# A piece of layer 1 moved behind the weight sums in TensorE's order (graph attention, two layers, one core)

## The chip, the core and the metric

The kernel runs on one core of a Trainium2 chip. A core has a matrix engine (TensorE, PE in the profile; its weight loads are the row PEld), a vector engine (VectorE, DVE), a scalar engine (ScalarE, ACT), GpSimd (POOL) and SyncE (SP), which here issues transfers, and 16 DMA engines. The engines run beside each other, each through its own list of instructions in order; they wait for each other on semaphores. The metric is the device time of one execution in microseconds (us); lower is better.

## What is computed

`x` is 4096 x 512, `adj` a 4096 x 4096 matrix of zeros and ones. Two graph layers follow, each with a residual and a layer norm:

```python
# layer 0: graph attention, 8 heads of 64
feats = einsum('nf,hfo->hno', x, W)
dense = leaky_relu(s_self[:, :, None] + s_neigh[:, None, :], 0.2) * A
out   = einsum('hij,hjo->hio', softmax(dense), feats) + b
x     = layernorm(x + relu(out as 4096 x 512))
# layer 1: attention inside 32 graphs of 128 nodes
scores = (where(mask, q @ k.T * scale, 0) + adj + adj) * where(mask, 1, -1e6)
x      = layernorm(x + (softmax(scores) * mask) @ v)
```

## The kernel before

**Layer 0 as a stream.** The exponential of a leaky ReLU of a sum is one of two products, so a weight can be had from a maximum of two terms. The kernel passes over the transposed adjacency four times, `main_pass(r)` with r = 0 to 3, two heads in each. A pass has four chunks c = 0 to 3 of 1024 rows, a chunk 32 tiles j of 128 neighbours. The tiles go in cycles: 8 tiles a cycle in passes 0 to 2 (`wide=8`), 4 in the last pass (r = 3). Chunks and cycles are numbered from 0 here. For each j and head, DVE makes `q` (line 1369, 128 x 1024), and ACT (line 1378) or, once in four tiles, DVE (line 1374) makes `mark`, which says on which side of the maximum an entry lies.

A cycle on PE is, in the order of the code:

- `accf` (line 1389): the products of the adjacency tile with the features f ("A f"), 16 matmuls for 4 tiles;
- a first call of `pieces`, place 0 (only where r > 0);
- `acc` (line 1409): the products of `q` with the scaled features g ("Q g"), 64 matmuls for 4 tiles, four side by side on 32 columns each;
- a second call of `pieces`, place 1;
- `dens` (line 1423): the weight sums from the marks, 32 matmuls for 8 tiles, so only in cycles that end on a multiple of 8;
- in pass 0 `ae` (`sums_over_a`, line 1333), and then the rest of the adjacency tiles of the next cycle (`bring`): in pass 0 transposes on PE into a `ps_m` bank (line 1115), copied out by ACT (line 1119) and written to DRAM by POOL; in later passes a load on SP's queue (line 1105).

**Pieces.** Other work on PE is cut into generators and run at these two places. When a chunk ends, `sums_to_rows` takes the sums out (DVE lines 1163 and 1171 empty `accf` and `acc`, ACT line 1173 copies `dens`) and gives a generator that turns them into rows. In passes 0 to 2 `run_pieces` steps it: in pass 0 at place 1, in passes 1 and 2 at place 0. For pass 0 it has three steps with PE work: `pz` (4 transposes, line 1186, read by DVE lines 1191 and 1197), `pd` (line 1220, read by line 1223) and `fin` (8 transposes into two banks, line 1243, read by line 1244).

In the last pass, from chunk 1 on, `run_plan` steps layer 1 itself for the blocks of the chunk before, by a plan written out by hand (lines 1277 and 1278). In its strings E is the generator of the chunk that ended, a and b are the two blocks of 512 rows, R loads the rows of the second, F ends a layer norm. The plan of cycle g is a pair, place 0 and place 1:

```python
PLAN = [("E", "b"), ("b", "Fb"), ("b", "a"), ("Ra", "a"), ("Fa", "b"), ("ba", "b")]
PLANS = PLAN + [("ab", ""), ("aaba", "")], PLAN + [("a", ""), ("aa", "a")]
```

`layer_1` has nine steps: two of transposes of the rows (line 960, copied to `x1T` by ACT, line 961); two of zT = M x (line 980, sixteen matmuls each, copied by ACT line 987); the scores (line 1007) with their softmax; values 0 and 1 (line 1052) with a transpose between; rows out (line 1066, then DVE line 1068 and a layer norm); values 2 and 3 (line 1052, sixteen matmuls, read by DVE line 1060); rows out.

**Order and buffers.** Only PE's order is the order of the code; for the other engines a planner fixes the order when the program is built, from the order of the code and its own estimate of when operands are ready:

```python
ctx.enter_context(tc.manual_schedule(engines={mybir.EngineType.PE}))
```

PSUM has eight banks: `acc` 2, `accf` 2, `dens` 1; in pass 0 `ae` 1 and two `ps_m` banks that all pieces and `bring` share in turn, later three `ps_m` banks. `q` has 8 buffers in passes 0 to 2, 6 in the last; marks have 18.

Of the kernel before, what the change touches and what calls it, by code (L numbers as in the profile page):

```python
# [404 lines left out]
def adjacency_streamed_path(  # L405
# [152 lines left out]
    def ring(name, pool, n):  # L558

        if name not in more:  # L560
            return pool
        k = turns[name] % (n + more[name][1])
        turns[name] += 1
        return pool if k < n else more[name][0]
# [536 lines left out]
    def bring(r, c, j):  # L1101

        if r:
            at = ats[r, c, j] = ring("at", atp, 6).tile([P, C], F32R, name="at")
            nc.sync.dma_start(at.bitcast(F32), at_d[c, j])
            return
        if j % 2:
            return
        if j % 4 == 0 and (c, j) not in a_bs:
            load_adjacency(c, j)  # L1110
        pairs = a_bs[c, j - j % 4].rearrange("p t n -> p (t n)").bitcast(BF16)
        pairs = pairs.rearrange("p (t k n) -> p t k n", t=CT, k=2)[:, :, j % 4 // 2, :]
        pt = misc([P, CT, P], BF16)
        for t in range(CT):
            nc.tensor.transpose(pt[:, t, :], pairs[:, t, :], ident_b)  # L1115
        both = pt.rearrange("p t n -> p (t n)").bitcast(FP8).rearrange("p (n k) -> p n k", k=2)
        for k in range(2):
            at = ats[r, c, j + k] = ring("at", atp, 6).tile([P, C], F32R, name="at")
            nc.scalar.copy(at, both[:, :, k])  # L1119
            nc.gpsimd.dma_start(at_d[c, j + k], at.bitcast(F32))  # L1120

    def load_block():

        k = len(checked)
        per = N // CK
        if k < per * NT:
            ck = ckp.tile([P, CK], F32, name="ck")
            nc.sync.dma_start(ck, adj[ts(k // per, P), ts(k % per, CK)])
            checked.append(ck)
# [151 lines left out]
    def run_plan(todo, pinned=False):  # L1281
        for k in todo:
            if k == "F":
                plan[k](pinned)
                continue
            gen = ends[0] if k == "E" else plan[k]
            if gen is not None:
                next(gen)
            if k == "E":
                ends.pop(0)  # L1290
# [3 lines left out]
    def run_pieces(budget):  # L1294

        state["credit"] += budget
        while state["credit"] > 0.0 and (work or ends):
            queue = ends or work
            try:
                state["credit"] -= next(queue[0])  # L1300
            except StopIteration:
                queue.pop(0)
        if not (work or ends):
            state["credit"] = 0.0
# [3 lines left out]
    def main_pass(r, ae=None, wide=4):  # L1308

        for c in range(NCH):  # L1310
# [10 lines left out]
            def pieces(c, group, place):  # L1321
                if r == PR - 1 and c:
                    run_plan(PLANS[c == NCH - 1][group][place])
                elif place == (r == 0):
                    run_pieces(0.75 * wide)
# [18 lines left out]
            for j0 in range(0, NT, wide):  # L1344
                at_step = steps.index((r, c, j0))
                cycle = range(j0, j0 + wide)
                f_s, g_s = {}, {}
                for k in range(j0 // 4, (j0 + wide) // 4):
                    f_s[k] = fsp.tile([P, 4, 2, FP], F32R, name="f_s")
                    nc.sync.dma_start(  # L1350
                        f_s[k].rearrange("p u s n -> p (u s n)").bitcast(F32), f_d[r, k]
                    )
                    g_s[k] = gfp.tile([P, 4, 2, FH], F32, name="g_s")
                    nc.sync.dma_start(g_s[k].rearrange("p u h o -> p (u h o)"), g_d[r, k])
                if at_step == 0:
                    for j in cycle:
                        bring(0, 0, j)
                follow = [
                    x
                    for x in steps[at_step + wide : at_step + 2 * wide]  # L1360
                    if x[0] == r or x[0] < PR - 1 or x[2] < 4
                ]
                qs = {}
                for j in cycle:
                    for h in range(2):
                        hh = 2 * r + h
                        q = qs[j, h] = ring("q", qp, 6).tile([P, C], F32, name="q")
                        d_j = d_all[:, j, hh : hh + 1]
                        nc.vector.scalar_tensor_tensor(  # L1369
                            q, p_row[h], d_j, ats[r, c, j].bitcast(F32), op0=OP.max, op1=OP.mult  # L1370
                        )
                        mark = marks[j, h] = sgp.tile([P, C], FP8, name="mark")
                        if j % 4 == 3 and h == 1:
                            nc.vector.tensor_scalar(  # L1374
                                mark, q, d_j, None, op0=OP.is_gt, saturate=False
                            )
                        else:
                            nc.scalar.activation(  # L1378
                                mark,
                                q,  # L1380
                                AF.Sigmoid,
                                bias=nb_all[:, j, hh : hh + 1],
                                scale=BIG,
                                saturate=False,
                            )
                for j in cycle:
                    for w in range(2):
                        for s in range(2):
                            nc.tensor.matmul(  # L1389
                                accf[:, s, :],  # L1390
                                f_s[j // 4][:, j % 4, w, :],
                                ats[r, c, j][:, ts(s, HB)],
                                start=(j == 0 and w == 0),
                                stop=(j == NT - 1 and w == 1),
                            )
                if r == 0 and (c, j0 + wide) == (NCH - 1, NT):

                    sums_over_a(c, cycle)
                first = wide // 2 if r == 0 or wide == 4 else 6
                for x_ in follow[:first]:  # L1400
                    bring(*x_)
                if r:
                    pieces(c, j0 // 4, 0)

                for j in cycle:
                    for s in range(2):
                        for o in range(0, FP, 32):
                            h = o // FH
                            nc.tensor.matmul(  # L1409
                                acc[o : o + 32, s, :],  # L1410
                                g_s[j // 4][:, j % 4, h, o % FH : o % FH + 32],
                                qs[j, h][:, ts(s, HB)],
                                start=(j == 0),
                                stop=(j == NT - 1),
                            )
                pieces(c, j0 // 4, 1)

                done_j = j0 + wide
                for j in range(done_j - 8, done_j) if done_j % 8 == 0 else ():
                    for s in range(2):  # L1420
                        for h in range(2):
                            lo = 32 * (2 * s + h)
                            nc.tensor.matmul(  # L1423
                                dens[lo : lo + 6, :],
                                e_b[:, j, 2 * r + h, :],
                                marks[j, h][:, ts(s, HB)],
                                start=(j == 0),
                                stop=(j == NT - 1),
                            )
                if r == 0 and (c, j0 + wide) != (NCH - 1, NT):  # L1430
                    sums_over_a(c, cycle)
                for x_ in follow[first:]:
                    bring(*x_)
                group_0 = (at_step - NT * NCH) // 4
                for group in range(group_0, group_0 + wide // 4) if r else ():
                    if group == 0:
                        load_block()
                        load_block()
                    for _ in range(1 + (group % 3 == 2)):
                        check_block(done[0])  # L1440
                        done[0] += 1
                        load_block()
# [16 lines left out]
    with tc.tile_pool(name="wl1", bufs=1, side="right") as wp:  # L1459
# [4 lines left out]
        for gen in work:  # L1464
            for _ in gen:
                pass
        work.clear()
    main_pass(2, wide=8)
    more.clear()
    wide_passes.close()  # L1470
# [60 lines left out]
```

## Time and profile before

| what | us |
|---|---|
| three runs | 2071.25, 2072.22, 2074.30 |
| median | 2072.22 |
| the profiled execution, its own time | 2073.38 |
| its span, first to last instruction | 2071.1 |
| pass 0 to pass 2, start to end | about 169 to 1366 |
| last pass, chunk 0 | 1366 to 1462 |
| last pass, chunks 1 to 3, and the tail | 1462 to 1952, 1952 to 2071 |

The busy shares of the engines and the granted clock of PE in parts of the execution:

| from : to | PE busy | DVE busy | ACT busy | clock |
|---|---|---|---|---|
| 316 : 343 (a cycle of pass 0) | 26.66 | 22.07 | 23.06 | 1.00 |
| 1366 : 1462 | 96.00 | 89.92 | 87.02 | 1.00 |
| 1462 : 1631 | 167.36 | 127.11 | 118.75 | 1.00 |
| 1631 : 1802 | 170.64 | 127.72 | 110.01 | 1.00 |
| 1802 : 1952 | 150.00 | 114.05 | 95.78 | 1.00 |

A row of a timeline is: start in us, length in us, engine, line, operation, what is written from what, shape, and how many are merged (x16). A bracket gives the idle time of the engine before it and whose result ended it. Matmul records overlap, so the time that a block of them takes on PE is read from its own start to the start of the next block.

### The profile page before, as it was taken

To read this page: it belongs to the slowest core of one execution; us is meant where nothing else is said; L and a number is where in the kernel's file an instruction comes from. 1 tells how busy PE (TensorE), PEld (TensorE's weight loads), DVE (VectorE), ACT (ScalarE), POOL (GpSimd) and SP (SyncE) were. 2 spreads that over 40 slices of the span, in tenths; PEclk is the share of its full clock that TensorE was granted. 3 is DMA by queue.
4 is the path that set the end of the run, shared out by engine and by line. 5 is a ranking of instruction groups with operands and counts; after the bars stand their busy time and mean duration, and the time that the engine had idled before them with its cause. 6 is when DMAs were issued, how large, how long until landed. Compare 5 with 4: busy or idle time off the path is not lost.

```text
span 2071.1 us, 37984 instructions
## 1 busy us (share of the span) xinstructions
PE 2038.5 (98%) x14934; PEld 1000.2 (48%) x14934; DVE 1664.2 (80%) x2058; ACT 1536.9 (74%) x1821; POOL 249.3 (12%) x393
## 2 busy tenths in 40 slices
PE   8999999999999999999999999999999999999997
PEld 4555555445445444444445444544454444445453
DVE  5557888888899998798999999999975984886654
ACT  3338898888878899788899889998885666567420
POOL 2333222222100000000000000000210210210111
PEclk9999999999999999999999999999999999999999
DMA  8999999999899999889999999989974774674211
GB/s 250 264 261 247 271 293 265 296 263 291 267 335 345 359 346 333 261 311 294 326 310 338 308 346 330 328 286 366 314 247 143 244 249 128 228 274 168 72 49 43
DMA packets 207881, 551.28 MB, mean 266 GB/s; under 512 B 25292, under 2 KB 66252, under 8 KB 207692
## 3 DMA queue, kind: packets, MB, share of 16 engines
q1 hardware_dynamic: 140748, 425.79, 59.3%
q0 software_dynamic: 62784, 121.91, 23.5%
q8 instruction: 119, 1.95, 0.4%
q10 hardware_dynamic: 4160, 1.05, 0.2%
q14 instruction: 70, 0.57, 0.1%
HBM read 491.79 MB, written 107.22 MB: 289 GB/s over the span
## 4 chain that ended last, share of the span: by engine, by line
PE 88%; DMA 5%; DVE 3%; issue 2%; ACT 1%; POOL 0%; SPq 0%; POOLq 0%; DVEq 0%; ACTq 0%
PE acc L1409 38%; PE accf L1389 22%; PE ps_m L1052 5%; PE dens L1423 5%; PE ps_m L980 5%; PE ps_set L736 4%; DMA at_d<-at 2%; DVE q L1369 2%; DMA a_b<-in_adj_dram 2%; PE ps_m L1007 1%; PE ps_m L1066 1%; PE ps_m L1115 1%; DMA xt_f<-in_x_dram 1%; PE ps_m L960 1%; PE ps_m L909 1%
## 5 line engine op out<-in xcount | busy, mean ns | idle before, releaser
L1369 DVE SCALAR_TENSOR_TENSOR q<-p_row,d_all,at 128x1024 f32<-128x1024 f32 x1024 | 1242.5, 1280 | 159.2 <-PE acc L1409 130.0
L1378 ACT ACTIVATE mark<-q,nb_all 128x1024 fp8e4<-128x1024 f32 x896 | 994.8, 1145 | 175.6 <-DVE q L1369 160.3
L1409 PE MATMUL acc<-q,g_s 128*32 128x512 f32 x8192 | 902.9, 593 | 1.1 <-DVE q L1369 0.4
L1409 PEld LDWEIGHTS acc<-q,g_s 128*32 128x32 f32 x8192 | 264.4, 110 | 594.3 <-issue 532.1
L1389 PE MATMUL accf<-at,f_s 128*128 128x512 f32 x2048 | 492.7, 396 | 1.8 <-issue 1.8
L1389 PEld LDWEIGHTS accf<-at,f_s 128*128 128x128 f32 x2048 | 379.2, 188 | 110.0 <-issue 29.1
L1134 ACT ACTIVATE ck<-ck,neg_half_f 128x1024 f32<-128x1024 f32 x128 | 146.0, 1140 | 18.9 <-DMA ck<-in_adj_dram 18.9
L1135 ACT ACTIVATE ck<-ck,neg_quarter 128x1024 f32<-128x1024 f32 x128 | 146.3, 1143 | 1.8
L1119 ACT CAST at<-ps_m 128x1024 fp32r<-128x1024 fp8e4 x128 | 120.2, 1025 | 8.6 <-PE ps_m L1115 5.6
L1423 PE MATMUL dens<-mark,e_b 128*6 128x512 fp8e4 x2048 | 124.4, 379 | 1.1 <-ACT mark L1378 1.1
L736 PE MATMUL ps_set<-w_sb_f,xT_f 128*128 128x512 f32 x256 | 116.0, 600 | 0.9 <-DMA w_sb_f<-in_L_gnn_W_dram 0.8
L1052 PE MATMUL ps_m<-wvT,x1T 128*128 128x512 f32 x256 | 114.2, 594 | 0.0
L980 PE MATMUL ps_m<-x1T,M_sb 128*128 128x512 f32 x256 | 113.0, 595 | 0.9 <-ACT x1T L961 0.9
L1254 POOL DMA_DIRECT2D hs_d<-hst x12 | 10.7, 894 | 834.1 <-DVE hst L1244 740.1
L1374 DVE TENSOR_SCALAR mark<-q,d_all 128x1024 fp8e4<-128x1024 f32 x128 | 96.0, 750 | 5.0 <-DVE q L1369 0.5
L1423 PEld LDWEIGHTS <-e_b 128*6 128x6 bf16 x2048 | 52.9, 86 | 80.7 <-issue 37.7
L1120 POOL DMA_DIRECT2D at_d<-at x128 | 69.1, 540 | 172.7 <-ACT at L1119 104.4
L758 ACT ACTIVATE fst<-fb 128x512 fp32r<-128x512 f32 x32 | 20.4, 637 | 84.3 <-DVE fb L744 50.9
L980 PEld LDWEIGHTS ps_m<-x1T,M_sb 128*128 128x128 f32 x256 | 48.0, 190 | 62.6 <-issue 60.4
L1052 PEld LDWEIGHTS ps_m<-wvT,x1T 128*128 128x128 f32 x256 | 47.6, 190 | 57.2 <-issue 56.0
L987 ACT ACTIVATE zT<-ps_m,zb 128x512 f32<-128x512 f32 x32 | 21.8, 682 | 71.0 <-PE ps_m L980 71.0
L736 PEld LDWEIGHTS ps_set<-w_sb_f,xT_f 128*128 128x128 f32 x256 | 48.6, 198 | 51.6 <-issue 50.2
(185 smaller groups left out, 1121.0 us busy)
## 6 DMA issues: line engine op xcount, KB each, us to landing
at<-at_d SPq DMA_DIRECT2D x384, 512.0 KB, 6.0
ck<-in_adj_dram SPq DMA_DIRECT2D x128, 512.0 KB, 5.4
f_s<-f_d SPq DMA_DIRECT2D x128, 512.0 KB, 7.4
at_d<-at POOLq DMA_DIRECT2D x128, 512.0 KB, 15.2
g_s<-g_d SPq DMA_DIRECT2D x128, 256.0 KB, 5.6
f_d<-fst POOLq DMA_DIRECT2D x32, 512.0 KB, 8.6
p_row<-pu_d SPq DMA_DIRECT2D x32, 512.0 KB, 6.7
a_b<-in_adj_dram POOLq DMA_DIRECT2D x32, 512.0 KB, 17.1
```

The costliest lines, as they stand in the source:

```text
L736: nc.tensor.matmul(pf, tile_j(xTs[k][:, c].rearrange("p u n -> p (u n)"), u), w_sb[:, c, :], start=(c == 0), stop=(c == FC - 1),)
L980: nc.tensor.matmul(pz, L1["M"][:, f, ts(c, P)], x1T[:, f, :], start=(f == 0), stop=(f == FC - 1),)
L1052: nc.tensor.matmul(pv, x1T[:, f, ts(u, P)], L1["wvT"][:, f, :], start=(f == 0), stop=(f == FC - 1),)
L1119: nc.scalar.copy(at, both[:, :, k])
L1134: tc.keep_in_program_order(nc.scalar.activation(ck, ck, AF.Square, bias=neg_half))
L1135: nc.scalar.activation(ck, ck, AF.Abs, bias=neg_quarter, accum_out=binp[:, k : k + 1])
L1369: nc.vector.scalar_tensor_tensor(q, p_row[h], d_j, ats[r, c, j].bitcast(F32), op0=OP.max, op1=OP.mult)
L1374: nc.vector.tensor_scalar(mark, q, d_j, None, op0=OP.is_gt, saturate=False)
L1378: nc.scalar.activation(mark, q, AF.Sigmoid, bias=nb_all[:, j, hh : hh + 1], scale=BIG, saturate=False,)
L1389: nc.tensor.matmul(accf[:, s, :], f_s[j // 4][:, j % 4, w, :], ats[r, c, j][:, ts(s, HB)], start=(j == 0 and w == 0), stop=(j == NT - 1 an ...
L1409: nc.tensor.matmul(acc[o : o + 32, s, :], g_s[j // 4][:, j % 4, h, o % FH : o % FH + 32], qs[j, h][:, ts(s, HB)], start=(j == 0), stop=(j ...
L1423: nc.tensor.matmul(dens[lo : lo + 6, :], e_b[:, j, 2 * r + h, :], marks[j, h][:, ts(s, HB)], start=(j == 0), stop=(j == NT - 1),)
```

## The change

The call of `pieces` at place 1 moves from in front of the `dens` matmuls to behind them. In pass 0 it then stands ahead of `sums_over_a`; in all passes it stays ahead of the second half of the `bring` calls.

```diff
@@ -1413,8 +1413,6 @@
                                 start=(j == 0),
                                 stop=(j == NT - 1),
                             )
-                pieces(c, j0 // 4, 1)
-
                 done_j = j0 + wide
                 for j in range(done_j - 8, done_j) if done_j % 8 == 0 else ():
                     for s in range(2):
@@ -1427,6 +1425,7 @@
                                 start=(j == 0),
                                 stop=(j == NT - 1),
                             )
+                pieces(c, j0 // 4, 1)
                 if r == 0 and (c, j0 + wide) != (NCH - 1, NT):
                     sums_over_a(c, cycle)
                 for x_ in follow[first:]:
```

The function that it calls is unchanged:

```python
def pieces(c, group, place):
    if r == PR - 1 and c:
        run_plan(PLANS[c == NCH - 1][group][place])
    elif place == (r == 0):
        run_pieces(0.75 * wide)
```

## The prediction

> **What bounds the kernel.** I read the page first: the span, the busy shares and the chain that ended last.
>
> ```profile
> span 2071.1 us, 37984 instructions
> PE 2038.5 (98%) x14934; PEld 1000.2 (48%) x14934; DVE 1664.2 (80%) x2058; ACT 1536.9 (74%) x1821; POOL 249.3 (12%) x393
> PE 88%; DMA 5%; DVE 3%; issue 2%; ACT 1%; POOL 0%; SPq 0%; POOLq 0%; DVEq 0%; ACTq 0%
> ```
>
> TensorE (PE) has 88% of the chain, so a step of PE's order is worth what it changes in PE's own row. But matmul records overlap, and 98% busy proves little; what counts is the distance from one block's first matmul to the next block's. So I went on to the timeline of PE around one moved piece (last pass, chunk 1, cycle 5: columns are start, length, then what):
>
> ```profile
> 1550.72 7.07 PE L1409 MATMUL acc<-q,g_s 128*32 128x512 f32 x64
> 1557.72 7.13 PE L980 MATMUL ps_m<-x1T,M_sb 128*128 128x512 f32 x16
> 1564.79 1.90 PE L1423 MATMUL dens<-mark,e_b 128*6 128x512 fp8e4 x32
> 1566.62 3.96 PE L1389 MATMUL accf<-at,f_s 128*128 128x512 f32 x16
> 1570.42 1.02 PE L1052 MATMUL ps_m<-wvT,x1T 128*128 128x512 f32 x2
> ```
>
> The starts give 7.00 + 7.07 + 1.83 + 3.80 = 19.70 us with no wait marked. PE's waits summed over the last pass (1462 to 1952) are only 0.9 us on ACT's x1T and 0.4 us on q. PE is the bound there, and there is little waiting to win.
>
> [...] The even starts speak for PE, and the sum goes by them.
>
> **What the change moves.** The call at place 1 goes behind `dens`. It does so in more places than the few words say: `pieces` runs work at place 1 where the pass is the last and c > 0, and also where `place == (r == 0)`, that is, in pass 0. `dens` runs only in cycles whose end is a multiple of 8. So the plan lists give in the last pass: "Fb" in cycle 1, "a" in cycle 3, "b" in cycle 5 of chunks 1 to 3, and "a" in cycle 7 of chunk 3. In chunk 1's cycle 1 b is still None. That leaves eight pieces of sixteen 128x512 matmuls (cycles 3 and 5 of chunk 1; 1, 3 and 5 of chunks 2 and 3) and one `rows_out` (L1066). In pass 0, where each cycle of 8 ends with `dens`, chunks 1 to 3 have three pieces each: `pz`, `pd` and the two `fin` tiles of the previous chunk: nine. No DMA is emitted between the two places, so the order on SP's queue keeps; what the pieces issue themselves (the write of `hs_d`, the output rows, both POOL) stays ahead of the same transfers.
>
> **Last pass, order alone.** Where `dens` follows `acc` directly, the profile shows it in chunk 1's cycle 7:
>
> ```profile
> 1609.43 7.07 PE L1409 MATMUL acc<-q,g_s 128*32 128x512 f32 x64
> 1616.32 1.91 PE L1423 MATMUL dens<-mark,e_b 128*6 128x512 fp8e4 x32
> ```
>
> 6.89 us against 7.00. `dens` then a piece is 1.83 (1948.99 to 1950.82), and the piece behind it 6.97 (1950.82 to 1957.79) up to another f32 block. A piece followed directly by `accf` stands at one kind of place:
>
> ```profile
> 1635.91 3.60 PE L1052 MATMUL ps_m<-wvT,x1T 128*128 128x512 f32 x8
> 1638.94 4.20 PE L1389 MATMUL accf<-at,f_s 128*128 128x512 f32 x16
> 1642.98 1.88 PE L1066 MATMUL ps_m<-v_t,pT_f 128*128 128x512 f32 x4
> ```
>
> Eight take 3.03 there and 3.43 elsewhere (1967.29 to 1970.72), -0.40, and `accf` 4.04. After: 6.89 + 1.83 + (6.97 - 0.40) + 4.04 = 19.33, so -0.37 each, -3.0 for eight. The `rows_out` place: before 7.01 + 1.91 + 1.83 + 6.97 = 17.72, after 6.89 + 1.83 + 1.81 + 6.87 = 17.40: -0.3.
>
> **Last pass, a wait filled.** Chunk 1's cycle 3 is the one place where the piece waits:
>
> ```profile
> 1514.94 7.11 PE L980 MATMUL ps_m<-x1T,M_sb 128*128 128x512 f32 x16 [0.85 <-ACT x1T L961]
> ```
>
> With `dens` in front, 1.83 us of work covers the 0.85: -0.85. Does `dens` then wait for marks? Its last four matmuls, some 1.6 us into it, read the newest mark. In the nine places ACT's and DVE's marks end between 1.2 us before and 0.8 us after the last start of `acc`, and that start is 0.4 us ahead of `dens`. The tightest is chunk 3's cycle 5: mark ends 1900.78, needed about 1902.0. So nothing is lost, with 1.2 us to spare there and 1.6 to 3.2 elsewhere. The moved pieces' readers have time: zT's banks are wanted 7 us later at the least, v_t is written over 1.5 us ahead of the `rows_out` that reads it, and in the tail the output rows' DVE work shifts 1.8 us into a gap of 2.66 us (DVE idle before 1961.93).
>
> Last pass in all: -3.0 - 0.3 - 0.85 = -4.1.
>
> **Pass 0.** Order alone: before, 321.62 - 307.75 = 13.87, then 0.59, 1.72 and 1.02; after, 13.76 (281.95 to 295.71), 1.83, 0.44 to 0.59, 1.01: between -0.16 and 0. I take -0.1, nine times: -0.9. The cost is on the other side, in who empties the bank:
>
> ```profile
> 321.62 0.66 PE L1186 MATMUL ps_m<-ident_f,hst 128*128 128x128 f32 x4
> 322.21 1.90 PE L1423 MATMUL dens<-mark,e_b 128*6 128x512 fp8e4 x32
> 323.93 1.09 PE L1333 MATMUL ae<-at,e_p 128*25 128x512 bf16 x16
> 325.91 0.62 PE L1115 MATMUL ps_m<-ident_b,a_b 128*128 128x128 bf16 x8 [0.34 <-DVE hst L1197]
> ```
>
> ```profile
> 321.21 2.48 DVE L1369 SCALAR_TENSOR_TENSOR q<-p_row,d_all,at 128x1024 f32<-128x1024 f32 x2
> 323.60 0.16 DVE L1191 TENSOR_REDUCE n<-ps_m 128x4 f32<-128x8 f32 x1
> 325.50 0.35 DVE L1197 TENSOR_REDUCE hst<-ps_m 128x96 f32<-128x192 f32 x1
> ```
>
> `pz` is complete about 322.25, yet DVE reads it at 323.60: two q of the next cycle stand ahead in DVE's order, which is fixed before the run (only PE's is written by hand, line 455). PE's second `bring` already waits for that reader (0.34 us marked), and behind it the whole PE queue, `accf` first. With `dens` in front the transposes come 1.7 us later. If DVE's order stays, it waits from 323.60 to about 323.95: +0.35 at each `pz`. If the planner sees the late operand, it puts more q (1.2 us each) ahead of the reader. The `fin` piece is the same with another victim: L1244 and then L1163, which empties `accf`; at the end of pass 0 PE already waits for that:
>
> ```profile
> 590.65 1.90 PE L1423 MATMUL dens<-mark,e_b 128*6 128x512 fp8e4 x32
> 594.32 7.59 PE L1389 MATMUL accf<-at,f_s 128*128 128x512 f32 x32 [1.76 <-issue]
> 592.93 1.28 DVE L1163 SCALAR_TENSOR_TENSOR ys<-accf,S_col,u_row 128x1024 f32<-128x1024 f32 x1
> ```
>
> Bounds, by the number of further q ahead of the readers: none, 3 x 0.35 + 2 x 0.25 + 0.35 = +1.9; one, 3 x 1.2 (`pz`) + 2 x 1.1 + 1.2 (`fin`; 0.1 of cover at two) = +7.0, `pd` free because its bank is read in 0.3 us and wanted 1.3 us after; two, 3 x 2.4 + 2 x 2.3 + 2.4 + 3 x 0.9 (`pd`) = +16.9. The delay, 1.7 to 1.8 us, is 1.45 q long, so I interpolate: 7.0 + 0.45 x 9.9 = +11.5. Part is absorbed: in chunk 2, `dens` at 401.89 takes 3.38 us instead of 1.73 since ACT's marks are late; a later PE meets them ready: -1.6.
>
> **Sum:** -4.1 - 0.9 + 11.5 - 1.6 = +4.9 on the profiled execution, 2073.38 us with 2.28 outside its span, 1.16 above the runs' median. On the median 2072.22: 2077.1.
>
> **Rivals.**
> A (forecast, 0.52): one to two further q ahead of the readers in pass 0. One gives +0.4, two +10.3: 2072.6 to 2082.5.
> B (0.24), not slower: DVE's order in pass 0 stays and its reader only waits: -5.0 + 1.9 = -3.1, or -4.7 with the wait absorbed: 2067.5 to 2069.1. For it: DVE has 4 to 5 us idle in each 26 us cycle (22 busy of 27 in 316 to 343). Against: q is ready there and a planner seldom lets an engine wait.
> C (0.10), faster: the pass 0 work finds a slot that costs nothing, or the change acts in the last pass alone, as its words say: -5.0, 2067.2. Against: line 1324.
> D (0.14), slower by another way: ACT's order changes in the last pass, so that a pair of block checks (L1134 and L1135, 2.3 us) stands ahead of the last mark, and `dens`, now directly behind `acc`, waits. It decides from 1.2 us of lateness (chunk 3's cycle 5); one pair in every place costs what it exceeds the nine margins by, 2.4 us in all, two pairs 21.6. The middle, 12.0, with B's terms: -3.1 + 12.0 = +8.9, 2081.1. For it: ACT is 64 to 70% busy there; against: in cycle 7, without a piece, `dens` never waits.
>
> **How the numbers follow.** The runs differ by 0.15%, so 0.2%, 4.1 us, is about what can be told from no change. A, spread over its bounds, lies above +4.1 in two of three: slower 0.34 + 0.14 (D) = 0.48; faster: half of B and C, 0.22; the same: 0.18 + 0.12 = 0.30. The likeliest is A's middle, 2077.1, its own range 2072.6 to 2082.5. The range reaches to C below and a little over A's end above, 2067 to 2084.
>
> **What would show it.** In the last pass: `acc` to `dens` 6.89, no mark wait at `dens`, L980 without the 0.85 us. In pass 0: three or four q between DVE's mark and L1191, the second `bring` waiting 1.5 us and more for L1197, and `accf` later at each chunk's start. I am wrong if pass 0 keeps its length, or if PE waits for marks in the last pass.

## The result, and the profile after

The changed kernel takes 2089.75 us (median of six runs, 2086.09 to 2093.13) beside 2071.64 us for the kernel before in the same session (six runs, 2070.67 to 2074.3): a ratio of 1.0085, 95% interval 1.0073 to 1.0097. It is slower, as forecast, but by 18.1 us where the forecast had 4.9, and outside its range. The profiled execution of the changed kernel took 2087.56 us, 14.2 us more than the one before.

In the page of the changed kernel the busy shares hardly move; that PE's busy time grew by only 2 us while the span grew by 14.1 says that PE now stands still more:

```profile
span 2085.2 us, 37978 instructions
PE 2040.5 (98%) x14934; PEld 1007.9 (48%) x14934; DVE 1664.4 (80%) x2058; ACT 1539.0 (74%) x1821; POOL 246.3 (12%) x393
```

To place the loss I took the start of `acc` in every cycle of both traces and subtracted. The changed kernel is behind by 19.3 us when pass 1 begins, keeps that through passes 1 and 2 (19.3 at the start of the last pass, 19.7 at that of its chunk 1), then gains 3.4 us over the cycles of the last pass up to chunk 3's cycle 5, 0.3 us at the `rows_out` place, and 2.0 us in the tail. So pass 0 pays everything. By place, in us (the column "marks" is the first cycle of chunk 2, where `dens` now meets its marks ready; chunk 3's `fin` is the end of pass 0, with the wait for `accf` behind it):

| pass 0 | `pz` | `pd` | `fin` | marks |
|---|---|---|---|---|
| chunk 1 | +4.00 | +1.01 | +2.31 | |
| chunk 2 | +3.73 | +0.99 | +2.25 | -2.08 |
| chunk 3 | +2.41 | +0.98 | +3.86 | |

The timeline of the changed kernel shows the mechanism at chunk 1's `pz`, first on VectorE, then on TensorE (start, length, instruction, wait in brackets):

```profile
320.42 0.74 DVE L1374 TENSOR_SCALAR mark<-q,d_all 128x1024 fp8e4<-128x1024 f32 x1
321.08 4.86 DVE L1369 SCALAR_TENSOR_TENSOR q<-p_row,d_all,at 128x1024 f32<-128x1024 f32 x4
325.86 0.15 DVE L1191 TENSOR_REDUCE n<-ps_m 128x4 f32<-128x8 f32 x1
...
327.76 0.35 DVE L1197 TENSOR_REDUCE hst<-ps_m 128x96 f32<-128x192 f32 x1
```

```profile
321.37 1.91 PE L1421 MATMUL dens<-mark,e_b 128*6 128x512 fp8e4 x32
323.21 0.66 PE L1186 MATMUL ps_m<-ident_f,hst 128*128 128x128 f32 x4
323.80 1.09 PE L1333 MATMUL ae<-at,e_p 128*25 128x512 bf16 x16
324.82 0.62 PE L1115 MATMUL ps_m<-ident_b,a_b 128*128 128x128 bf16 x8
328.16 0.66 PE L1115 MATMUL ps_m<-ident_b,a_b 128*128 128x128 bf16 x8 [2.72 <-DVE hst L1197]
328.59 5.73 PE L1389 MATMUL accf<-at,f_s 128*128 128x512 f32 x17
```

The transposes of `pz` (L1186) are done at 323.87, but VectorE reads them at 325.86: four q stand between its mark and the reader, where two stood before. The second `bring` needs the bank, so PE waits 2.72 us for L1197 (before: 0.34), and behind it everything. All nine readers in pass 0 have four q ahead in the new order. PE's waits in pass 0 of the changed kernel, from 176 us on (us in total, times, longest):

```profile
PE ps_m L1115 <- DVE hst L1197: 8.2, 3, 2.7
PE accf L1389 <- issue: 4.3, 1, 4.3
PE ps_m L1115 <- DVE hst L1244: 2.5, 2, 1.3
PE ps_m L1115 <- DVE parts L1223: 2.4, 3, 0.8
PE accf L1389 <- DVE ys L1163: 1.2, 2, 0.6
```

"issue" is a wait whose end the profile does not name; it ends when VectorE has emptied `accf` (L1163 ends at 612.05, `accf` starts at 612.16) at the end of pass 0.

The last of the PE rows shows one more thing: the 17 `accf` matmuls behind the wait take 5.73 us, 0.34 each, where 16 took 3.96 us in the row of before, 0.25 each. The windows of the changed kernel (stretch in us, its length, PE busy and matmul count, granted clock, DMA share and GB/s) show the granted clock beside it: for a while it is 0.50, half of full speed. Its half-clock stretches inside pass 0 are 3.41 us long, and the pairs below are the stretch ahead of each of them and the stretch itself, then the third `pz`, where there was none:

```profile
325.21:328.62 3.41, 0.69 (x14) 1.00 1.07 365
328.62:332.03 3.41, 3.41 (x11) 0.50 1.02 418
437.85:441.26 3.41, 1.08 (x20) 1.00 0.99 396
441.26:444.68 3.42, 3.02 (x13) 0.50 0.56 220
608.51:611.93 3.42, 0.00 (x0) 1.00 0.98 303
611.93:615.34 3.41, 3.18 (x8) 0.50 0.89 267
550.49:553.90 3.41, 1.70 (x26) 1.00 1.02 413
553.90:557.31 3.41, 2.41 (x17) 1.00 0.63 244
```

After a stretch with 0.69, 1.08 or 0 us of PE work the clock is halved for the next stretch; after one with 1.70 us it is not, although the third `pz` waits 2.71 us like the other two. The steps in the table agree: `pz` costs 4.00 and 3.73 where the clock fell, 2.41 where it did not.

The last pass did what it should. Chunk 1's cycle 5 of the changed kernel:

```profile
1569.21 7.07 PE L1409 MATMUL acc<-q,g_s 128*32 128x512 f32 x64
1576.10 1.91 PE L1421 MATMUL dens<-mark,e_b 128*6 128x512 fp8e4 x32
1577.94 7.13 PE L980 MATMUL ps_m<-x1T,M_sb 128*128 128x512 f32 x16
1584.51 4.24 PE L1389 MATMUL accf<-at,f_s 128*128 128x512 f32 x16
1588.58 3.60 PE L1052 MATMUL ps_m<-wvT,x1T 128*128 128x512 f32 x8
```

6.89 + 1.84 + 6.57 + 4.07 = 19.37 us, against 19.70 before. The 0.85 us wait at chunk 1's cycle 3 is gone too.

### The profile page after: what moved, and what is told of

It is laid out like the page before. It is cut to its first block, busy times and chain, and to the rows that moved or that the text cites. A ratio compares the mean times of both kernels' runs of the same rounds, so it can differ in the third digit from the quotient of the medians.

```text
span 2085.2 us, 37978 instructions
## 1 busy us (share of the span) xinstructions
PE 2040.5 (98%) x14934; PEld 1007.9 (48%) x14934; DVE 1664.4 (80%) x2058; ACT 1539.0 (74%) x1821; POOL 246.3 (12%) x393
## 4 chain that ended last, share of the span: by engine, by line
PE 92%; DVE 4%; DMA 2%; issue 1%; ACT 0%; POOL 0%; SPq 0%; POOLq 0%; DVEq 0%; ACTq 0%
PE acc L1409 41%; PE accf L1389 23%; PE ps_m L1052 5%; PE dens L1421 5%; PE ps_m L980 5%; PE ps_set L736 4%; DVE q L1369 3%; PE ps_m L1007 1%; PE ps_m L1115 1%; PE ps_m L1066 1%; DMA xt_f<-in_x_dram 1%; PE ps_m L960 1%; PE ps_m L909 1%; PE ps_m L1243 1%; PE ps_set L654 1%
## 5 line engine op out<-in xcount | busy, mean ns | idle before, releaser
L1389 PE MATMUL accf<-at,f_s 128*128 128x512 f32 x2048 | 499.3, 401 | 5.4 <-issue 4.3
L1389 PEld LDWEIGHTS accf<-at,f_s 128*128 128x128 f32 x2048 | 383.8, 190 | 114.3 <-issue 31.7
L1060 DVE TENSOR_TENSOR v_t<-ps_m,bv_row 128x512 f32<-128x512 f32 x32 | 21.8, 685 | 60.6 <-PE ps_m L1052 60.6
```

What stands on the lines that cost most here:

```text
L1389: nc.tensor.matmul(accf[:, s, :], f_s[j // 4][:, j % 4, w, :], ats[r, c, j][:, ts(s, HB)], start=(j == 0 and w == 0), stop=(j == NT - 1 an ...
```

## The experiments

Theory: all the loss is in pass 0, and its cause is VectorE's fixed order, which lets further q in front of the readers; a part is the clock that falls after long waits. The rivals: the last pass takes part in it; the later place of the transposes costs by itself, whatever VectorE does; the clock falls without regard to the waits. Times are medians; the kernel before was run beside each group: 2072.33 us (29 runs) for the first four, 2073.39 us (11 runs) for the kernel with the call behind `ae`, the first run with filler and the kernel with one q fewer, 2074.93 us (11 runs) for the two runs made side by side.

**The last pass alone.**

```diff
+                if r == 0:
+                    pieces(c, j0 // 4, 1)
                 done_j = j0 + wide
...
-                pieces(c, j0 // 4, 1)
+                if r:
+                    pieces(c, j0 // 4, 1)
```

> Only the last pass has the new order; pass 0 keeps the old one, and VectorE keeps two q between its mark and the readers there. Theory (the whole loss sits in pass 0; the last pass gains 1.22 + about 8 x 0.33 = 3.9 us): about 2067.8 us (2066 to 2069.5), pass 1 begins as early as before. Rival (the last pass gives its gain back, for instance in the tail): 2071 us or more.

2068.3 us (11 runs), ratio 0.9980 (0.9971 to 0.9990): faster than the kernel before by 4.0 us. The order in pass 0 keeps two q ahead of the readers. In the trace the lag falls by 1.22 us at chunk 1's cycle 3 and by 0.29 to 0.33 at the seven other places, as in the changed kernel. The rival falls.

**Pass 0 alone.** The same edit with the two conditions exchanged.

> Only pass 0 has the new order; the last pass is as before. Theory: the changed kernel plus the lost 3.9 us of the last pass, about 2093.5 us (2090 to 2097), pass 1 begins 18 to 20 us later than before, four q between VectorE's mark and all nine readers. Rival (part of the loss sits in the last pass): below 2086 us.

2092.27 us (5 runs), ratio 1.0089 (1.0076 to 1.0102). Pass 1 begins 19.5 us later than before, and its places cost what they cost in the changed kernel, but for where the clock fell: here the first `pz` (+4.01), the first `fin` (+3.87) and the end of pass 0 (+3.94), not the second `pz` (+2.38). So in the traces the two halves of the change add up, and the last pass has no share in the loss. By the medians they give -4.0 + 19.9 = +15.9 us, where the changed kernel itself lost 18.1 and, in its second group of runs below, 15.4.

**The changed place, with VectorE's order held.** PE's order is that of the changed kernel; in pass 0 every q of the next cycle from the fourth on is tied behind the reader, so that two stand between VectorE's mark and the reader, as in the kernel before.

```diff
+                        behind = ExitStack()
+                        if (j, h) > (j0 + 1, 0) and "reader" in last:
+                            behind.enter_context(tc.issue_after(last["reader"].ins))
+                        with behind:
                             nc.vector.scalar_tensor_tensor(
                                 q, p_row[h], d_j, ats[r, c, j].bitcast(F32), op0=OP.max, op1=OP.mult
                             )
```

(`last["reader"]` is the reader traced last in pass 0: the second L1197, L1223 or L1244, whose lines are up to 2 further down in this kernel; it is cleared after the q of a cycle.)

> The changed kernel, but VectorE's order in pass 0 is held: all q of the next cycle from the fourth on are tied behind the reader, so that again only two q stand between its mark and the readers L1191, L1223 and L1244. TensorE's order is the changed one. Theory (VectorE's order is what costs): pass 0 then pays +1.9 for readers that wait for their operands and gets back 0.9 for the order and 2.1 for the marks, so -1.1; with the last pass -3.9 the sum is -5.0, about 2066.6 us (2064.5 to 2070), no wait over 0.9 us for L1197 in pass 0 and no half-clock window there. Rival (the place itself costs, since the transposes stand later in TensorE's order whatever VectorE does): pass 1 begins 10 us or more later than before, 2078 us or more.

2071.76 us (12 runs, 2068.25 to 2076.0), ratio 0.9993 (0.9984 to 1.0001): level with the kernel before, 18 us better than the changed kernel, 5 us above what the theory expected. The timeline of this kernel at the same `pz`, VectorE and then TensorE:

```profile
321.17 2.47 DVE L1378 SCALAR_TENSOR_TENSOR q<-p_row,d_all,at 128x1024 f32<-128x1024 f32 x2
323.99 0.17 DVE L1191 TENSOR_REDUCE n<-ps_m 128x4 f32<-128x8 f32 x1 [0.36 <-PE ps_m L1186]
```

```profile
323.30 0.66 PE L1186 MATMUL ps_m<-ident_f,hst 128*128 128x128 f32 x4
323.89 1.09 PE L1338 MATMUL ae<-at,e_p 128*25 128x512 bf16 x16
324.90 1.07 PE L1115 MATMUL ps_m<-ident_b,a_b 128*128 128x128 bf16 x16
325.78 7.55 PE L1399 MATMUL accf<-at,f_s 128*128 128x512 f32 x32
```

The transposes are as late as in the changed kernel, VectorE waits 0.36 us for them, and PE waits for nothing: up to the third `pz` this kernel is 0.6 us ahead of the kernel before, where the changed one is 14.5 behind. So the place itself costs nothing there, and VectorE's order is the cause. That the total is not 2066.6 has one seen reason: at the end of pass 0 the planner put three small instructions (L832, L833 and L836, 591.16 to 591.99) in front of L1244, PE waits 2.61 us for `accf`, and the clock is halved behind it from 595.4 on (the 32 `accf` matmuls take 9.18 us there, 7.59 in the kernel before); that place costs 2.3 us. Another 4.6 us are lost in the profiled execution, the slowest of the twelve, before chunk 1 of the last pass: 1.4 us in pass 1, in a wait for a load of `f_s`, and 3.2 us in chunk 0 of the last pass, 0.6 of them in a wait for q. The first kernel with filler, which is as in the changed kernel there, loses 2.9 us in the same chunk, so this need not come from the ties; it is not explained.

**Half way.** The last pass as before; in pass 0 the piece stands in the middle of the weight sums.

```diff
                 for j in range(done_j - 8, done_j) if done_j % 8 == 0 else ():
+                    if r == 0 and j == done_j - 4:
+                        pieces(c, j0 // 4, 1)
```

> The last pass as before; in pass 0 the piece stands in the middle of the weight sums, behind 16 of their 32 matmuls, and VectorE's order then has three q ahead of the readers, one more than before. Theory (a whole q more ahead of each reader): about 3 x 1.2 + 2 x 1.1 + 1.2 = +7.0, less 0.5 to 2 for marks that are met ready: 2076 to 2079 us, waits for L1197 of 1.4 to 1.7 us, no half-clock window in pass 0. Rival 1 (cost in proportion to the delay of the transposes, half of the loss of the changed kernel's pass 0): about +9.6, 2081 us. Rival 2 (the loss is mostly the clock that drops after waits near 2.7 us): +3 or less, 2074 us or less.

2078.34 us (12 runs), ratio 1.0026 (1.0017 to 1.0035). VectorE's order has three q at all nine readers, one more than before:

```profile
320.55 3.67 DVE L1369 SCALAR_TENSOR_TENSOR q<-p_row,d_all,at 128x1024 f32<-128x1024 f32 x3
324.13 0.15 DVE L1191 TENSOR_REDUCE n<-ps_m 128x4 f32<-128x8 f32 x1
```

`pz` costs 1.18, 1.16 and 1.20 us, `pd` 0.02 at most, `fin` 1.14, 1.10 and 1.18, the marks give 2.09 back: +4.9 in the profiled execution, with waits for L1197 of about 1.5 us and no half clock in pass 0 (the mean clock of the execution is 0.997). The transposes come 0.98 us later here (the first 16 matmuls of the sums, 320.84 to 321.82), less than a q, and still a whole q goes in front; half the loss of the changed kernel's pass 0 would have been 9.6.

**Behind the `ae` matmuls too.** The last pass as before; in pass 0 the call stands one step further back.

```diff
                 if r == 0 and (c, j0 + wide) != (NCH - 1, NT):
                     sums_over_a(c, cycle)
+                if r == 0:
+                    pieces(c, j0 // 4, 1)
```

> The last pass as before; in pass 0 the piece stands behind the weight sums and behind the 16 ae matmuls, and VectorE has three further q ahead of eight of the nine readers (the ninth two). Theory (by the steps measured for one and two further q: pz 1.18 and 2.4, pd 0 and 0.98, fin 1.12 and 2.28, each further q adds 1.2): pz 3 x 3.6 + pd 3 x 2.2 + fin 2 x 3.5 + 2.3 = 26.7, less 2.1 for the marks, plus three to six half-clock windows of up to 1.7 us: +28 to +34, 2100 to 2106 us. Rival (the loss ends with what VectorE can run ahead, or with the one bank conflict): under +22, 2094 us or less.

2109.97 us (4 runs), ratio 1.0176 (1.0160 to 1.0191): more than expected. PE's long waits in pass 0 of this kernel, from 176 us on:

```profile
PE ps_m L1115 <- DVE hst L1197: 12.4, 3, 4.1
PE ps_m L1115 <- DVE parts L1223: 6.6, 3, 2.2
PE ps_m L1115 <- DVE hst L1244: 5.2, 2, 2.6
PE accf L1389 <- issue: 4.4, 1, 4.4
```

The order has three further q at eight readers and two at the ninth, and the waits are those of a third step: 4.1 for `pz`, 2.2 for `pd`, 2.6 for `fin` (1.3 with two). What was undersized is the clock: half clock stands behind all nine places (the mean granted clock is 0.51 in 328.70 : 332.11 behind `pz` and in 359.42 : 362.83 behind `pd`, and 0.989 over the execution beside 0.994 in the changed kernel), where I had three to six stretches of it. The steps of this trace add up to 38.4 us; less the 24.6 us that I had for waits and marks, 13.8 are left, 1.5 for each of the nine.

**Filling the wait.** The changed kernel with matmuls of zero weights in the place where PE waits for L1197.

```diff
                 for x_ in follow[first:]:
+                    if r == 0 and c and j0 == 8 and x_[2] == j0 + 14:
+                        for t in range(10):
+                            for j in (j0 + 4, j0 + 5):
+                                a_j = ats[r, c, j].bitcast(BF16).rearrange("p (n k) -> p n k", k=2)
+                                for s in range(2):
+                                    lo = 32 * (2 * (j % 2) + s)
+                                    nc.tensor.matmul(
+                                        ae[lo : lo + 7, :],
+                                        e_p[:, j, NE + 1 : 32],
+                                        a_j[:, ts(s, HB), 1],
...
                     bring(*x_)
```

> The changed kernel with 40 further matmuls of 0.068 us (2.7 us, weights of zero, so they add zero to the sums) in front of the second bring of the three cycles with pz: TensorE works there where it waited 2.7 us for L1197, and the wait's end does not move. Theory (a stretch of 3.41 us on a fixed grid, in which TensorE is busy for under about half, is followed by one at half clock, which costs up to 1.7 us): no half-clock window at these three places, pass 1 begins 16 to 17 us later than before instead of 18 to 20, and the median is some 2 to 3 us below that of the changed kernel with the same last pass, 2086 to 2088 us. Rival (the clock has nothing to do with the waits): as many half-clock windows as without, 2089 to 2093 us, and later by what the 40 matmuls overlap with.

2085.8 us (5 runs), ratio 1.0057 (1.0043 to 1.0071). At chunk 1's `pz`:

```profile
325.87 2.45 PE L1438 MATMUL ae<-at,e_p 128*7 128x512 bf16 x40
328.67 0.62 PE L1115 MATMUL ps_m<-ident_b,a_b 128*128 128x128 bf16 x8 [0.35 <-DVE hst L1197]
```

The second `bring` starts 3.35 us after the first, as in the changed kernel (3.34), but the clock stays up (the 22 `accf` matmuls behind it take 5.28 us, 0.24 each): `pz` costs 2.42, 2.38 and 2.41 us, and pass 1 begins 16.5 us later than before. Since that run and the changed kernel's were made in different groups, I put both on one chip:

> The changed kernel once more, for a comparison on one chip with the kernel that has the filler matmuls. Theory: about 1.0085 times the kernel before, and in its trace a half-clock window behind one to three of the three pz waits, just where the stretch of 3.41 us in front of it has TensorE busy under about 47 per cent, and none where it is over 50. Rival (windows fall without regard to how busy a stretch was): at least one window behind a stretch busier than that, or a stretch of under 40 per cent without one.

> The changed kernel with the 40 filler matmuls, beside the changed kernel itself on the same chip. Theory: 2 to 4 us less than the changed kernel (two or three half-clock windows of 1.3 to 1.7 us each gone), no window at the three pz places. Rival (the difference between the two earlier runs came from the chip): within 1 us of the changed kernel.

The changed kernel: 2090.32 us (5 runs), ratio 1.0077 (1.0062 to 1.0093). With the filler: 2086.0 us (6 runs), ratio 1.0059 (1.0044 to 1.0073). 4.3 us lie between the medians, a little over the upper end of what was expected; the intervals of the two ratios overlap, but both pairs of runs point the same way. The traces are clearer. In the changed kernel the stretches ahead of the three `pz` waits' ends have:

```profile
325.20:328.61 3.41, 0.69 (x13) 1.00 1.11 323
437.84:441.25 3.41, 1.21 (x20) 1.00 1.02 408
550.48:553.89 3.41, 1.77 (x26) 1.00 1.03 414
```

The first two are followed by half clock (`pz` +4.01 and +3.68), the third is not (+2.37). With the filler none is (+2.42, +2.34, +2.41). At the end of pass 0, which has no filler, the clock drops in all of these kernels (in the profile of the changed kernel above to 0.50 in 611.93 : 615.34, behind a wait of 4.25 us).

**One q fewer.** The kernel of the first experiment (the new order in the last pass alone), with the ties of the third one from a q earlier on, `(j, h) > (j0, 1)`, so that one q stands ahead of the readers at the old place.

> The order of the best kernel so far (the new order in the last pass alone), and in pass 0, at the old place, the q from the third on tied behind the reader, so that one q stands ahead of the readers where there were two. Theory (a q less ahead of each reader is worth what PE waits for it): the three waits of 0.34 us for L1197 go, -1.0, and the 1.8 us wait at the end of pass 0 shrinks by 0.4 (a q of 1.2 less, three small instructions of 0.8 us more): about 2066.9 us (2064.5 to 2069). Rival (the q tied behind come late for acc, or the ties disturb later orders): 2069 us or more.

2067.61 us (7 runs), ratio 0.9972 (0.9961 to 0.9983). The waits for L1197 are gone and that at the end of pass 0 is 1.3 us: by the starts of `acc`, the three `pz` and the end of pass 0 take 0.5 us less each than in the kernel before. But `dens` now waits longer for its marks, in this kernel (first two rows) and in the kernel before (third):

```profile
PE dens L1433 <- ACT mark L1387: 3.2, 5, 0.7
PE accf L1399 <- issue: 1.3, 1, 1.3
PE dens L1423 <- ACT mark L1378: 1.1, 2, 0.7
```

With these waits the first cycles of chunks 2 and 3 take 0.9 and 2.5 us more, and pass 0 as a whole is 1.3 us longer than before. So the waits for the readers can be taken away, but that the order costs the kernel before anything on balance is not shown. This and the first experiment's kernel beat both kernels; the two can't be told apart by their intervals.

## Why the prediction was right in its sign and wrong in its size

**Last pass, -4.1 predicted, -3.7 measured.** Chunk 1's cycle 3 gave 1.22 us, as worked out (0.37 + 0.85), the `rows_out` place 0.30, as worked out, and the seven others 0.29 to 0.33 each instead of 0.37. `dens` never waited for a mark there, so D did not happen. The tail gave a further 2.0 us that no step held: in the profiled execution of before a half-clock stretch stood there (granted clock 0.50 from 2000.7 to 2004.1), in the changed kernel's none, and the wait ahead of it was 0.5 us longer. The transposes in question, before and after:

```profile
1999.31 2.43 PE L960 MATMUL ps_m<-ident_f,x1b 128*128 128x128 f32 x16 [2.20 <-DVE x1b L528]
2014.87 1.99 PE L960 MATMUL ps_m<-ident_f,x1b 128*128 128x128 f32 x16 [1.73 <-DVE x1b L528]
```

Whether the order has a part in that is open: this wait is 1.5 to 2.2 us in the four traces with the old order in the last pass and 1.2 to 1.8 us in the seven with the new one, and half clock follows it in three of the four and in one of the seven (the tied kernel's).

**Pass 0, the step that failed.** The bounds were right as far as they went, without the clock; the choice between them was wrong. "The delay, 1.7 to 1.8 us, is 1.45 q long, so I interpolate: 7.0 + 0.45 x 9.9 = +11.5" treats the number of further q as a mean. It is a whole number, the same at all nine readers: one for a delay of 0.98 us, two for the 1.84 us of the change, three with the `ae` matmuls in between too (2.74 us), and two at the one reader where no `ae` lies between. A q is 1.2 us; in these orders the count is the delay in q (0.8, 1.5, 2.3), rounded up. That the planner rounds is read from the orders; its rule was not looked into. The bound for two was +16.9; measured without the clock, `pz` gave 3 x 2.4 = 7.2 (7.2 predicted), `pd` 3.0 (2.7), the two `fin` 4.6 (4.6), and the end 3.86 less a half-clock stretch of some 1.5 = 2.4 (2.4): 17.2. The bound for one, +7.0, less the order's 0.9 and the marks' 1.6, is 4.5; the half-way kernel's profiled execution has +4.9.

**A term that was missing.** No step held the clock. The changed kernel's profiled pass 0 loses 1.6 + 1.3 + 1.5 = 4.4 us to it. With 5.7 for the second q (17.2 - 11.5), 0.9 for the gain from PE's order alone, which the measured steps already hold, and less 0.5 since the marks gave 2.08 instead of 1.6, that makes 10.5, the difference between the 9.0 predicted for pass 0 and the 19.45 measured.

**The rivals.** B, VectorE's order stays and the reader only waits, is what the tied kernel builds: PE then waits for nothing at `pz`, so even its +0.35 each was too much. The tied kernel took 2071.76 us where B had 2067.5 to 2069.1. B's chance was too high, for by itself the order did not stay. C's time, 2067.2, is near that of the last pass alone, 2068.3. Of the signs that I had named, the wait of "1.5 us and more" and the four q were seen; `accf` was later at chunk starts too (two waits of 0.6 us for L1163).

**The median and the profiled execution.** The runs of the changed kernel spread over 7 us and go with their mean clock, 2093.13 us at 0.992 and 2086.09 at 0.995; the profiled one is 2.2 us under their median, that of before 1.7 us over its own (2073.38 to 2071.64). That is why 14.2 us in the profiles are 18.1 us in the medians.

## What to carry to other kernels

When a piece of work is moved on an engine whose order is written by hand, count where its readers go on the engine whose order is planned, in whole instructions and not as a mean between bounds, and look at what the reader releases: here a bank that the next matmuls wanted, so that a further q became up to 1.2 us of waiting. An edit that acts in two stages is costed and tried in each by itself: the last pass alone gains 4 us, pass 0 alone loses 20. Waits of 2 to 3 us on TensorE are costed with the clock that may fall behind them: here a wait of 2.7 us cost up to 1.6 us more by it.

## What the hardware showed beyond the forecast

The changes of TensorE's granted clock lie on a grid of 3.413 us in each of the eleven profiled executions: in the changed kernel half clock begins at 328.62, 441.26 and 611.93, 33 and 50 such steps apart. The grid stands differently to the program from run to run: 0.50 us behind the first instruction in the kernel before, 0.94 us in the changed one. I added up PE's busy time in each stretch of the grid from the traces, from 176 us to the last 15. 25 stretches at half clock follow one with 0 to 1.59 us of work; of those at full clock one follows 1.57 us and all others 1.64 or more. (Two more, at the end of pass 0, follow 2.18 and 2.73 us of work that was itself at half clock.) So in these traces half clock followed the stretches in which TensorE worked for less than about 1.6 of the 3.413 us, and a wait of 2.7 us cost up to 1.6 us more (`pz` +4.01 beside +2.38 in the kernel with pass 0 alone) or nothing, by how it fell on the grid: the second `pz` dropped in the changed kernel and not in the one with pass 0 alone.
